# Where the row maxima of two attentions are split into bf16 parts: GpSimd or VectorE, in a planned single-core Trainium2 kernel

## The chip, the cores and the metric

The kernel runs on one core of one Trainium2 chip. The metric is the device time of one execution in microseconds (us), as the median of several runs; lower is better. One further execution was recorded by the hardware profiler, and the profile and the trace are of that one.

## The reference, cut to what matters

The input is 4096 tokens of 256 channels. After a layer norm two branches run on it, and their results are added to the input.

```python
xn = _layernorm(x)
x = x + _L0_attn_ref(xn, ...) + _L0_ffn_ref(xn, ...)

# branch 1: global attention, 16 heads of 16 channels, 4096 x 4096 scores for each head
attn = einsum('bqhd,bkhd->bhqk', q, k);  sq = attn * attn
w = sq / (nsum - 2.0 * sq + EPS)                 # nsum = |q|^2 + |k|^2
out = softmax(w) @ v

# branch 2: two layers, each a local attention (window 128, 8 heads of 64) and a gated feed-forward part
sim = where(mask, -max, bq @ bk.T);  o = softmax(sim) @ bv;  x = x + o @ wo
h = layernorm(shift_token(x)) @ w1 + b1;  a, g = split(h);  x = x + (a * gelu(g)) @ w2 + b2
```

Both softmaxes subtract the maximum of each row before the exponential. The change concerns how this maximum gets from where it is found to where it is subtracted.

## The kernel before, in words

**Global attention.** A *tile* is 128 queries of one head against all 4096 keys: 16 heads x 32 = 512 tiles, each in two *halves* of 2048 keys, each half in two pieces of 1024. The path of a half:

1. `scores` (L951): PE multiplies Q and K into PSUM; `square` (L955): ACT squares into SBUF buffer `r`, of which there are 9 (`R_BUFS`).
2. `less` (L959): VectorE subtracts 1.
3. A reciprocal by logarithm and exponential on ACT (`log` L978, `power` L981), on `u` buffers, of which there are two (`U_BUFS`). A tile takes one of two forms: *paired*, where VectorE multiplies the two halves (`product` L963), takes an absolute value (`positive` L972) and, after one logarithm and one exponential, restores the sign (`signed` L985); or *unpaired*, with `positive`, `log` and `power` once for each half. The paired form has more VectorE work, the unpaired one more ACT work.
4. `weights` (L993): one VectorE instruction for each half multiplies and finds the row maximum, followed by a short instruction that reads the accumulator into `mm`.
5. `maximum` (L1002 to L1007): the maximum, one number for each of 128 queries, is turned into three bf16 parts. The upper half of its bits is the first part; GpSimd subtracts it from the maximum (L1007), the upper half of the rest is the second part, and a second subtraction leaves the third. After each part a DMA on the SP queue (L1004) writes it as a row of `mrow`.
6. `turn` (L1014, L1017): PE transposes `r` into PSUM, having first put the negated sum of the three rows of `mrow` there (L1014). `exp` (L1025) on ACT, `values` (L1036) on PE into `pv`.
7. After four tiles `copied` (L1043) copies `pv` to `ob`, and a DMA on SP stores `ob` (L1045).

Q is loaded for four tiles at a time (`load_q`, L338), with two buffers; the load for the next four is issued at the scores of the first of a four.

**Local attention and feed-forward.** This is one long generator, `ffn` (L596 on), of which each `yield step(engine, ns, ...)` names the engine and duration of the piece that follows. A group is 256 tokens, 16 groups in each of two layers. For each of four head pairs, `looked` (L716) computes the scores, masks and scales them with a row maximum on VectorE (L740, four instructions), has GpSimd split four maxima at once into three bf16 parts in `fm3` (L745 to L748), and issues three DMAs on SP into `frow` (L751); `summed` uses them on PE (L760). `fetch(g + 1)` loads the next group's `hT` and `tab` (L631 to L638). The feed-forward part follows with 512 tokens at a time (`shifted` loads them, L824), and `finals` computes the output rows.

**What sets the order.** PE, ACT and VectorE run in an order that a planner writes down while the kernel is built: `plan_all` adds tasks with an engine, an assumed duration in ns, what they wait for, which buffers they take and give, and a rank; `Plan.run` starts, on each free engine, the ready task of lowest rank. The ranks are the tile or half number plus an offset from `RANK` (S scores, Q square, and so on). Tasks of engine `X` are no engine's: their code is emitted when their time has come. The maximum is such a task:

```python
m = add("X", MAX_NS, lambda: acts.maximum(i), 2 * i, [w])
for n in (2 * i, 2 * i + 1):
    soft(n, m)
```

so that the turn of a tile is planned `MAX_NS` after its `weights`. `load` sums the planned ACT and VectorE work, and `paired = load[0] > load[1]` chooses the form of the next tile. `ffn` is paced along by `CHAIN_NS`. GpSimd and SP are not planned: their instructions stand in about the order in which the code is emitted, and each engine runs its own in order. An instruction at the head of SP's queue that waits for its source keeps all later ones waiting.

Of the kernel before, what the change touches and what calls it, by code (L numbers as in the profile page):

```python
# [23 lines left out]
NG = S // 512  # L24
# [12 lines left out]
U_BUFS = 2  # L37
PE_BUFS = 4
PRO_LIVE = 7
CHAIN_NS = 2.5755e6  # L40

# [3 lines left out]
AFTER = {"PE": 215.0, "ACT": 178.0, "DVE": 133.0, "X": 0.0}  # L47
MODE_NS = 97.0
MODE_BONUS = 1.0
MAX_NS = 6000.0  # L50
PACE = dict(PE=1.0, ACT=0.5, DVE=0.5, X=0.0)
RANK = dict(S=-8.0, Q=-3.0, D=-2.0, L=1.5, T=1.0, W=3.0, E=5.0, P=4.5, F=5.5, O=-20.0)


class Pool:
# [127 lines left out]
def plan_all(plan, acts, chain, halves):  # L183
# [7 lines left out]
    def rest(i, subs):  # L191
        paired = load[0] > load[1]
        load[0] += 10844 if paired else 14448
        load[1] += 12321 if paired else 9050
        acts.mode(i, paired)
        add, D, L, T = plan.add, 2 * i + RANK["D"], 2 * i + RANK["L"], 2 * i + RANK["T"]
        ready = []
        if paired:
            t = add("DVE", 2203, lambda: acts.product(i), D, subs, takes=[(U, i)])
            t = add("DVE", 1135, lambda: acts.positive(i, 0), D, [], [t])  # L200
            t = add("ACT", 1802, lambda: acts.log(i, 0), L, [t])
            t = add("ACT", 1802, lambda: acts.power(i, 0), L, [t])
            ready = [add("DVE", 2203, lambda: acts.signed(i), D, [t])] * 2
        else:
            for h in range(2):
                t = add("DVE", 1135, lambda h=h: acts.positive(i, h), D + h, [subs[h]], [t] if h else [], takes=[] if h else [(U, i)])
                p = add("ACT", 1802, lambda h=h: acts.log(i, h), L + h, [t])
                ready.append(add("ACT", 1802, lambda h=h: acts.power(i, h), L + h, [p]))
        w = None
        for h in range(2):  # L210
            w = add("DVE", 2255, lambda h=h: acts.weights(i, h), T + h, [ready[h]], [w], gives=[(U, i)] if h else [])
        m = add("X", MAX_NS, lambda: acts.maximum(i), 2 * i, [w])
        for n in (2 * i, 2 * i + 1):
            soft(n, m)

    def soft(n, m):
        i, half = divmod(n, 2)
        exps = []
        for z in range(2):
            w = plan.add("PE", 427 + 8 * 109, lambda z=z: acts.turn(n, z), n + RANK["W"] + 0.3 * z, [m], [last["W"]],  # L220
                         takes=[(PS, (n, z, 1))], gives=[(R, n)] if z else [])
            last["W"] = w
            e = plan.add("ACT", 905, lambda z=z: acts.exp(n, z), n + RANK["E"] + 0.3 * z, [w], takes=[(PE2, (n, z))], gives=[(PS, (n, z, 1))])
            exps.append(e)
        fresh = [last["copy"]] if half == 0 and i % 4 == 0 else []
        last["P"] = plan.add("PE", 874, lambda: acts.values(n), n + RANK["P"], exps + fresh, [last["P"]],
                             gives=[(PE2, (n, 0)), (PE2, (n, 1))], mode="C")
        if half and i % 4 == 3:
            last["copy"] = plan.add("ACT", 465, lambda: acts.copied(i), n + RANK["O"], [last["P"]])

    def begin(n):
        sq = []
# [40 lines left out]
def tile_yat_attention_and_local_ffn(ctx: ExitStack, tc: tile.TileContext, io, out):  # L273
# [322 lines left out]
    def ffn():  # L596
        for l in range(DEPTH):
# [63 lines left out]
            for g in range(NGF):  # L661
# [42 lines left out]
                for b in range(2):  # L704
# [4 lines left out]
                                 start=k == 0, stop=k == 1)  # L709
                    yield step("DVE", 600, give=True)  # L710
                    V.tensor_copy(va[:, (2 * g + b) % 3, :, 0:FD], pv.rearrange("p (h d) -> p h d", h=FH))
                if g + 1 < NGF:
                    nxt = fetch(g + 1)
                osum = fa.tile([128, 2, INNER], F32, name="xm2")

                def looked(c):  # L716

                    P = fb.tile([128, 2, 2, 256], F32, name="P")
                    mx = fb.tile([128, 4], F32, name="mx")

                    yield step("PE", 1200, "R", take=2)
                    pss = ps_s.tile([128, 2, 2, 256], F32, name=acts.name("pt", "f"))
                    for b in range(2):
                        t = 2 * g + b
                        s0, s1 = (t - 1) % 3, t % 3
                        for j in range(1 if s1 == s0 + 1 else 2):
                            for e in range(2):
                                r = 64 * e
                                lq = qT[r:r + 64, c, b * 128:(b + 1) * 128]
                                if s1 == s0 + 1:  # L730
                                    T.matmul(pss[:, e, b].rearrange("p (s n) -> p s n", s=2), lhsT=lq,
                                             rhs=kT[r:r + 64, c, s0:s0 + 2], start=True, stop=True)
                                else:
                                    T.matmul(pss[:, e, b, j * 128:(j + 1) * 128], lhsT=lq, rhs=kT[r:r + 64, c, (s0, s1)[j]],
                                             start=True, stop=True)
                    yield step("DVE", 1620, give=2)
                    for e in range(2):
                        for b in range(2):
                            mk = msk[:, 0 if (g == 0 and b == 0) else 1]
                            V.tensor_tensor_reduce(P[:, e, b], pss[:, e, b], mk, rn[:, 0, b, 2 * c + e:2 * c + e + 1], 3.0e38,  # L740
                                                   ALU.add, ALU.min, mx[:, 2 * e + b:2 * e + b + 1])
                    yield step("X", 0)
                    m3 = fb.tile([128, 3, 4], BF, name="fm3")
                    md = fb.tile([128, 4], F32, name="fmd")
                    G.tensor_copy(m3[:, 0], mx)  # L745
                    G.tensor_tensor(m3[:, 1], mx, m3[:, 0], ALU.subtract)
                    G.tensor_tensor(md, mx, m3[:, 0], ALU.subtract)
                    G.tensor_tensor(m3[:, 2], md, m3[:, 1], ALU.subtract)  # L748
                    mT = frow[c % 2]
                    for c_ in range(3):  # L750
                        nc.sync.dma_start(mT[c_:c_ + 1], m3[:, c_])  # L751
                    held[c] = P, mT, plan.now + 10000.0

                def summed(c):
                    P, mT, at = held.pop(c)
# [27 lines left out]
                for c in range(5):  # L783
                    if c < 4:
                        yield from looked(c)
                    if c:
                        yield from summed(c - 1)
                oT = fa.tile([128, 4, GT], F32, name="qT")
# [13 lines left out]
                yield step("DVE", 600, give=True)  # L802
                xm = fa.tile([128, 2, D], F32, name="xm")
                V.tensor_tensor(xm, pw, xres, ALU.add)
                nc.sync.dma_start(xm_d[l][g * GT + 1:(g + 1) * GT + 1].rearrange("(t p) c -> p t c", p=128), xm)

            if l == DEPTH - 1:
# [21 lines left out]
            for g in range(NG):  # L829
# [13 lines left out]
                hn = fa.tile([128, 4, D], F32, name="qT")  # L843
                for t in range(4):
                    V.tensor_scalar(hn[:, t], xh[:, t], mv[:, t, 0:1], rstd[:, t:t + 1], ALU.subtract, ALU.mult)
                if g + 1 < NG:
                    nxt = shifted(g + 1)
                h2 = []
                for c in range(2):
                    yield step("PE", 510, take=True)  # L850
# [3 lines left out]
                    yield step("DVE", 725, give=True)  # L854
                    h2.append(fb.tile([128, 512], F32, name="pT"))
                    V.tensor_scalar(h2[c], ph, lngb[:, 0, c:c + 1], lngb[:, 1, c:c + 1], ALU.mult, ALU.add)
                gg = fa.tile([128, 6, 512], F32, name="kv")

                def up(s_, m):
# [36 lines left out]
                if l < DEPTH - 1:  # L896
                    for c in range(2):
# [4 lines left out]
                        yield step("DVE", 600, give=True)  # L902
                        xoT = fb.tile([128, 512], F32, name="pT")
                        V.tensor_copy(xoT, ph)
                        for z in range(2):
                            nc.sync.dma_start(xT_d[l + 1][2 * g + z][c * 128:(c + 1) * 128], xoT[:, z * GT:(z + 1) * GT])
                    for z in range(2):
                        nc.sync.dma_start(xres_d[l + 1][2 * g + z].rearrange("(t p) c -> p t c", p=128), xo[:, 2 * z:2 * z + 2])
                else:
# [2 lines left out]
                    nc.sync.dma_start(xin, acc_d[g].rearrange("(t p) c -> p t c", p=128))  # L912
                    yield step("DVE", 1135)
                    V.tensor_tensor(xo, xo, xin, ALU.add)
                    nc.sync.dma_start(ff_d[g].rearrange("(t p) c -> p t c", p=128), xo)


# [5 lines left out]
    class Acts:  # L923
# [11 lines left out]
        def scores(self, n, z):  # L935
            i, half = divmod(n, 2)
            h, qt = tiles[i]
            if half == 0 and z == 0:
                if qt == 8 and h + 1 < H:
                    assert self.valued >= 8 * NT * h  # L940
                    load_k(h + 1)
                    load_v(h + 1)
                if qt % 4 == 0 and i // 4 + 1 < len(quads):
                    load_q(*quads[i // 4 + 1])
            if z == 0:
                self.r[n] = hr.tile([128, 2048], F32, name=self.name("r", n))
# [40 lines left out]
        def weights(self, i, h):  # L987

            if h == 0:
# [3 lines left out]
            V.tensor_tensor_reduce(self.r[2 * i + h], self.r[2 * i + h], self.part(i, h), 1.0 if self.paired[i] else -0.5, init,  # L993
                                   ALU.mult, ALU.max, self.mm[i][:, h:h + 1])
            if h:
                del self.u[i]

        def maximum(self, i):

            mm = self.mm.pop(i)  # L1000
            head = mm.bitcast(BF)
            self.mT[i] = mT = mrow[i % M_ROWS]  # L1002
            for c_ in range(1, 4):
                nc.sync.dma_start(mT[c_ - 1:c_, :], head[:, 2 * c_ + 1:2 * c_ + 2])  # L1004
                if c_ == 3:
                    break
                G.tensor_tensor(mm[:, c_ + 1:c_ + 2], mm[:, c_:c_ + 1], head[:, 2 * c_ + 1:2 * c_ + 2], ALU.subtract)  # L1007

        def turn(self, n, z):
            i, half = divmod(n, 2)  # L1010
# [29 lines left out]
        def copied(self, i):  # L1040
            h, qt = tiles[i]
            self.ob = hp.tile([128, 512], F32, name="ob", bufs=1)
            A.copy(self.ob, pav)  # L1043
            if i + 1 < len(tiles):
                nc.sync.dma_start(o_d[qt // 4][h], self.ob)  # L1045
                if h == H - 1:
# [178 lines left out]
```

## Time and profile before

| | |
|---|---|
| median of 3 runs | 7337.93 us (7336.72 to 7345.24) |
| the profiled execution | 7328.83 us, of which the span of its instructions is 7327.0 us |
| busy, share of the span | ACT 95%, VectorE (DVE) 94%, PE 92%, GpSimd (POOL) 25% |
| mean granted TensorE clock | 0.981 of full speed |
| L993, VectorE, 128x2048 | 1,024 instructions, mean 2346 ns (with a start value) and 2283 ns (without) |
| L1025, ACT, 128x1024 | 2,048 instructions, mean 1099 ns |
| L1007, GpSimd, 128x1 | 1,024 instructions, mean 1010 ns, 1033.9 us in all |
| L745, L746, L747, L748, GpSimd, 128x4 | 128 each, means 1695, 1587, 1570 and 1189 ns |

Busy time is the time in which an instruction of an engine was under way; on one engine the records of two successive instructions may overlap. Idle time has a releaser: what ended the wait, as semaphores show it. SPq is the queue of DMA issues of SyncE, DVE is VectorE, POOL is GpSimd, PEld is the weight load of PE. The local attention of the two layers runs from 288 to about 2620 us and from about 3620 to 5978 us, the feed-forward parts after each; the global attention runs all along from 240 us to the end.

### The profile page before, as it was taken

The numbers are of one execution on the slowest core, as the hardware profiler recorded it, in microseconds if no ns is written. First come the engines' busy times: TensorE is split into PE (matmuls) and PEld (weight loads), VectorE is DVE, ScalarE is ACT, GpSimd is POOL, SyncE is SP. The second block draws the span as 40 slices with busy tenths as digits, with TensorE's granted clock in tenths as the row PEclk, the third lists the DMA queues.
The fourth block names the chain that finished last, engine by engine and source line by source line (L and its number), as shares of the span: only waits on it lengthen the run. The fifth ranks groups of instructions, "written<-read, shape, count | busy, mean of one in ns | idle before, by whom it ended". The sixth has DMA issues, their size and how long they took to land. (4 is left out here: it accounts for less than half of the span.)

```text
span 7327.0 us, 158565 instructions
## 1 busy us (share of the span) xinstructions
PE 6747.6 (92%) x66274; PEld 4786.4 (65%) x67136; DVE 6907.5 (94%) x7307; ACT 6972.8 (95%) x6761; POOL 1806.4 (25%) x1567
## 2 busy tenths in 40 slices
PE   7799999999999998899999999999999999999998
PEld 3466666666676665666666676666666666666665
DVE  8999999999999998899999999999999999899998
ACT  8899999999999998899999999999999999899998
POOL 0123233223332322212223322332232220011210
PEclk9899999999999999999999999999999999999999
DMA  3201010010000111011110010101010023101012
GB/s 130 76 16 21 17 24 15 17 22 17 20 19 15 30 40 26 19 31 24 35 21 19 20 19 17 23 14 25 15 23 15 17 59 87 36 21 31 20 46 77
DMA packets 542303, 223.84 MB, mean 31 GB/s; under 512 B 374988, under 2 KB 514003, under 8 KB 539538
## 3 DMA queue, kind: packets, MB, share of 16 engines
q1 hardware_dynamic: 539650, 212.73, 12.3%
q8 instruction: 527, 8.63, 0.5%
q14 instruction: 190, 1.56, 0.1%
q10 hardware_dynamic: 1936, 0.92, 0.0%
HBM read 124.59 MB, written 88.08 MB: 29 GB/s over the span
## 5 line engine op out<-in xcount | busy, mean ns | idle before, releaser
L1017 PE MATMUL pt<-ident,r 128*128 128x128 f32 x16384 | 2497.5, 276 | 0.0
L1017 PEld LDWEIGHTS pt<-ident,r 128*128 128x128 f32 x16384 | 2082.7, 143 | 577.3 <-issue 199.4
L1025 ACT ACTIVATE pe<-pt 128x1024 f32<-128x1024 f32 x2048 | 2178.8, 1099 | 147.0 <-PE pt L1017 122.5
L955 ACT ACTIVATE r<-pt 128x1024 f32<-128x1024 f32 x2048 | 2120.9, 1104 | 86.5 <-PE pt L951 45.0
L1007 POOL TENSOR_TENSOR mm<-mm 128x1 f32<-128x1 f32 x1024 | 1033.9, 1010 | 4714.3 <-DVE mm L993 4547.7
L1014 PE MATMUL pt<-mrow,neg 128*128 128x512 bf16 x4096 | 1577.6, 385 | 220.8 <-DMA mrow<-mm 108.2
L978 ACT ACTIVATE u<-u 128x2048 f32<-128x2048 f32 x702 | 1395.4, 1997 | 26.8 <-DVE u L972 26.4
L981 ACT ACTIVATE u<-u 128x2048 f32<-128x2048 f32 x702 | 1403.5, 1999 | 0.7
L959 DVE TENSOR_SCALAR r<-r 128x2048 f32<-128x2048 f32 x1024 | 1242.5, 1221 | 65.2 <-ACT r L955 64.8
L993 DVE CUSTOM_DVE_ANT_0 r<-r,u,mm 128x2048 f32<-128x2048 f32 x512 | 1201.3, 2346 | 63.4 <-ACT u L981 58.4
L951 PE MATMUL pt<-K,Q 128*128 128x512 bf16 x3234 | 1013.2, 383 | 199.7 <-ACT pe L1025 129.8
L993 DVE CUSTOM_DVE_ANT_0 r<-r,u 128x2048 f32<-128x2048 f32 x512 | 1169.1, 2283 | 13.0 <-ACT u L981 6.4
L1036 PE MATMUL pv<-pe,vh 128*17 128x128 f32 x32768 | 1074.1, 275 | 21.4 <-ACT ob L1043 7.9
L1036 PEld LDWEIGHTS pv<-pe,vh 128*17 128x17 f32 x32768 | 819.0, 97 | 298.7 <-issue 279.7
L985 DVE SCALAR_TENSOR_TENSOR u<-u 128x2048 f32<-128x2048 f32 x322 | 736.1, 2286 | 74.6 <-ACT u L981 73.8
L951 PEld LDWEIGHTS <-Q 128*128 128x128 bf16 x4096 | 375.4, 99 | 574.6 <-issue 393.6
L963 DVE TENSOR_TENSOR u<-r,r 128x2048 f32<-128x2048 f32 x322 | 735.6, 2285 | 1.9
L1014 PEld LDWEIGHTS <-neg 128*128 128x128 bf16 x4096 | 406.7, 99 | 350.7 <-issue 249.6
L972 DVE TENSOR_SCALAR u<-r 128x2048 int32<-128x2048 int32 x380 | 457.1, 1219 | 1.6 <-DMA q_d<-pb 1.5
L972 DVE TENSOR_SCALAR u<-u 128x2048 int32<-128x2048 int32 x322 | 394.4, 1225 | 7.5
L863 PE MATMUL pf<-pT,wqkv_s 128*128 128x512 f32 (+1 forms) x768 | 367.5, 601 | 4.2 <-DVE kv L883 1.5
L745 POOL CAST fm<-mx 128x4 bf16<-128x4 f32 x128 | 216.9, 1695 | 481.2 <-DVE mx L740 470.5
(211 smaller groups left out, 6005.1 us busy)
## 6 DMA issues: line engine op xcount, KB each, us to landing
o<-ob SPq DMA_DIRECT2D x127, 256.0 KB
mrow<-mm SPq DMA_DIRECT2D x1536, 0.2 KB
Q<-q_d SPq DMA_DIRECT2D x256, 48.0 KB
K<-k_d SPq DMA_DIRECT2D x32, 384.0 KB
tab<-in_tables_dram SPq DMA_DIRECT2D x32, 256.0 KB
xres<-xres SPq DMA_DIRECT2D x32, 256.0 KB
xm<-xm SPq DMA_DIRECT2D x32, 256.0 KB
P<-xm SPq DMA_DIRECT2D x32, 256.0 KB
```

Of the source, the lines that this page charges most:

```text
L951: T.matmul(ps[:, j * 512:(j + 1) * 512], lhsT=Q[:, (qt % 4) * 128:(qt % 4 + 1) * 128], rhs=K[:, o + j * 512:o + (j + 1) * 512], start=True ...
L955: A.activation(self.r[n][:, z * 1024:z * 1024 + 1024], self.pt.pop((n, z)), AF.Square)
L959: V.tensor_scalar(self.r[n], self.r[n], 1.0, 1.0e-9, ALU.subtract, ALU.subtract)
L972: V.tensor_scalar(self.part(i, h).bitcast(I32), src.bitcast(I32), 0x7FFFFFFF, None, ALU.bitwise_and)
L978: A.activation(self.part(i, h), self.part(i, h), AF.Ln)
L981: A.activation(self.part(i, h), self.part(i, h), AF.Exp, scale=-2.0)
L993: V.tensor_tensor_reduce(self.r[2 * i + h], self.r[2 * i + h], self.part(i, h), 1.0 if self.paired[i] else -0.5, init, ALU.mult, ALU.max, ...
L1007: G.tensor_tensor(mm[:, c_ + 1:c_ + 2], mm[:, c_:c_ + 1], head[:, 2 * c_ + 1:2 * c_ + 2], ALU.subtract)
L1014: T.matmul(pt[:, 512 * b:512 * b + 512].rearrange("p (s n) -> p s n", s=4), lhsT=neg1, rhs=self.mT[i].unsqueeze(1).broadcast_to([128, 4, 1 ...
L1017: T.matmul(pt[:, 512 * b + j * 128:512 * b + (j + 1) * 128], lhsT=self.r[n][:, o + j * 128:o + (j + 1) * 128], rhs=ident, is_transpose=Tru ...
L1025: A.activation(pe, self.pt.pop((n, z)), AF.Exp)
L1036: T.matmul(pav[32 * (j % 4):32 * (j % 4) + 17, (qt % 4) * 128:(qt % 4) * 128 + 128], lhsT=vh[h % 2][:, kt, :], rhs=pe[:, j * 128:(j + 1) * ...
```

## The change

The bf16 parts of both maxima are made on VectorE, directly behind the instruction that finds the maximum: in `weights` two subtractions of 128x1 after the second half, in `looked` two subtractions of 128x4 and one copy of all twelve parts. GpSimd does nothing in either attention any more. The DMAs stay on SP. Several DMA issues move to a later place in the emitted order: the store of `ob` into a step of its own (`stored`), the next Q to the second tile of a four, `fetch(g + 1)` behind the second head pair, `shifted(g + 1)` behind the transposes, and the stores of `xm`, `xoT` and `ff` behind a step `X` that ends after the VectorE instruction that makes them. The planner's numbers follow: 145 ns for the pair and 240 ns for the three of `looked`, `MAX_NS` 5000 for 6000, ranks of S and Q lower, `CHAIN_NS` larger.

```diff
-CHAIN_NS = 2.5755e6
+CHAIN_NS = 2.6012e6
-MAX_NS = 6000.0
+MAX_NS = 5000.0
-RANK = dict(S=-8.0, Q=-3.0, D=-2.0, L=1.5, T=1.0, W=3.0, E=5.0, P=4.5, F=5.5, O=-20.0)
+RANK = dict(S=-13.0, Q=-3.5, D=-2.0, L=1.5, T=1.0, W=3.0, E=5.0, P=4.5, F=5.5, O=-20.0)
...
-        load[1] += 12321 if paired else 9050
+        load[1] += 12466 if paired else 9195
...
-            w = add("DVE", 2255, lambda h=h: acts.weights(i, h), T + h, [ready[h]], [w], gives=[(U, i)] if h else [])
+            w = add("DVE", 2255 + 145 * h, lambda h=h: acts.weights(i, h), T + h, [ready[h]], [w], gives=[(U, i)] if h else [])
...
             last["copy"] = plan.add("ACT", 465, lambda: acts.copied(i), n + RANK["O"], [last["P"]])
+            plan.add("X", 0, lambda: acts.stored(i), n, [last["copy"]])
...
-                if g + 1 < NGF:
-                    nxt = fetch(g + 1)
                 osum = fa.tile([128, 2, INNER], F32, name="xm2")
...
-                    mx = fb.tile([128, 4], F32, name="mx")
+                    mx = fb.tile([128, 3, 4], F32, name="mx")
...
-                    yield step("DVE", 1620, give=2)
+                    yield step("DVE", 1860, give=2)
...
+                    m3 = fb.tile([128, 3, 4], BF, name="fm3")
+                    hd = mx.bitcast(BF).rearrange("p j (n w) -> p j n w", w=2)[:, :, :, 1]
+                    for c_ in range(2):
+                        V.tensor_tensor(mx[:, c_ + 1], mx[:, c_], hd[:, c_], ALU.subtract)
+                    V.tensor_copy(m3, hd)
                     yield step("X", 0)
-                    m3 = fb.tile([128, 3, 4], BF, name="fm3")
-                    md = fb.tile([128, 4], F32, name="fmd")
-                    G.tensor_copy(m3[:, 0], mx)
-                    G.tensor_tensor(m3[:, 1], mx, m3[:, 0], ALU.subtract)
-                    G.tensor_tensor(md, mx, m3[:, 0], ALU.subtract)
-                    G.tensor_tensor(m3[:, 2], md, m3[:, 1], ALU.subtract)
                     mT = frow[c % 2]
                     for c_ in range(3):
                         nc.sync.dma_start(mT[c_:c_ + 1], m3[:, c_])
-                    held[c] = P, mT, plan.now + 10000.0
+                    held[c] = P, mT, plan.now + 8000.0
...
                         yield from looked(c)
+                    if c == 1 and g + 1 < NGF:
+                        nxt = fetch(g + 1)
...
                 V.tensor_tensor(xm, pw, xres, ALU.add)
+                yield step("X", 0)
                 nc.sync.dma_start(xm_d[l][g * GT + 1:(g + 1) * GT + 1].rearrange("(t p) c -> p t c", p=128), xm)
...
-                if qt % 4 == 0 and i // 4 + 1 < len(quads):
+                if qt % 4 == 1 and i // 4 + 1 < len(quads):
                     load_q(*quads[i // 4 + 1])
...
             if h:
+                mm, head = self.mm[i], self.mm[i].bitcast(BF)
+                for c_ in range(1, 3):
+                    V.tensor_tensor(mm[:, c_ + 1:c_ + 2], mm[:, c_:c_ + 1], head[:, 2 * c_ + 1:2 * c_ + 2], ALU.subtract)
                 del self.u[i]
...
             for c_ in range(1, 4):
                 nc.sync.dma_start(mT[c_ - 1:c_, :], head[:, 2 * c_ + 1:2 * c_ + 2])
-                if c_ == 3:
-                    break
-                G.tensor_tensor(mm[:, c_ + 1:c_ + 2], mm[:, c_:c_ + 1], head[:, 2 * c_ + 1:2 * c_ + 2], ALU.subtract)
...
+        def stored(self, i):
+            h, qt = tiles[i]
             if i + 1 < len(tiles):
                 nc.sync.dma_start(o_d[qt // 4][h], self.ob)
```

In the built programs the order on PE, ACT and VectorE is written anew by the planner throughout; the counts of PE's instructions and of SP's DMAs are the same, ACT has 32 more, VectorE 1,392 more, and GpSimd 36 instead of 1,572.

More of the change, by code (lines that the diff above doesn't have):

```diff
@@ L740, in looked @@
                             V.tensor_tensor_reduce(P[:, e, b], pss[:, e, b], mk, rn[:, 0, b, 2 * c + e:2 * c + e + 1], 3.0e38,
-                                                   ALU.add, ALU.min, mx[:, 2 * e + b:2 * e + b + 1])
-                    yield step("X", 0)
-                    m3 = fb.tile([128, 3, 4], BF, name="fm3")
-                    md = fb.tile([128, 4], F32, name="fmd")
-                    G.tensor_copy(m3[:, 0], mx)
-                    G.tensor_tensor(m3[:, 1], mx, m3[:, 0], ALU.subtract)
-                    G.tensor_tensor(md, mx, m3[:, 0], ALU.subtract)
-                    G.tensor_tensor(m3[:, 2], md, m3[:, 1], ALU.subtract)
+                                                   ALU.add, ALU.min, mx[:, 0, 2 * e + b:2 * e + b + 1])
+                    m3 = fb.tile([128, 3, 4], BF, name="fm3")
[3 more added lines that the diff above has]
+                    V.tensor_copy(m3, hd)
+                    yield step("X", 0)
                     mT = frow[c % 2]
@@ L845, in ffn @@
                     V.tensor_scalar(hn[:, t], xh[:, t], mv[:, t, 0:1], rstd[:, t:t + 1], ALU.subtract, ALU.mult)
-                if g + 1 < NG:
-                    nxt = shifted(g + 1)
                 h2 = []
@@ L856, in ffn @@
                     V.tensor_scalar(h2[c], ph, lngb[:, 0, c:c + 1], lngb[:, 1, c:c + 1], ALU.mult, ALU.add)
+                if g + 1 < NG:
+                    nxt = shifted(g + 1)
                 gg = fa.tile([128, 6, 512], F32, name="kv")
@@ L904, in ffn @@
                         V.tensor_copy(xoT, ph)
+                        yield step("X", 0)
                         for z in range(2):
@@ L914, in ffn @@
                     V.tensor_tensor(xo, xo, xin, ALU.add)
+                    yield step("X", 0)
                     nc.sync.dma_start(ff_d[g].rearrange("(t p) c -> p t c", p=128), xo)
```

## Prediction

> **What bounds the kernel now.** I read the page's busy line first, then the busy time by stretch, the waits, and three pieces of the timeline. Columns of the second fence: stretch and its length, then PE, PEld, DVE, ACT and POOL busy.
>
> ```profile
> PE 6747.6 (92%) x66274; PEld 4786.4 (65%) x67136; DVE 6907.5 (94%) x7307; ACT 6972.8 (95%) x6761; POOL 1806.4 (25%) x1567
> ```
>
> ```profile
> 300.00:2650.00 2350.00, 2194.10 (x22659) 1608.81 (x22949) 2264.48 (x2455) 2295.79 (x2279) 693.46 (x603) 0.99 0.10 20
> 2650.00:3600.00 950.00, 872.61 (x8099) 593.60 (x8201) 855.85 (x796) 873.68 (x772) 211.65 (x133) 0.97 0.11 26
> 3600.00:5900.00 2300.00, 2147.62 (x22210) 1577.17 (x22508) 2211.80 (x2380) 2244.65 (x2228) 659.21 (x585) 0.99 0.10 20
> 5900.00:7290.00 1390.00, 1288.19 (x12202) 877.38 (x12360) 1288.91 (x1226) 1309.09 (x1157) 229.16 (x214) 0.98 0.18 48
> ```
>
> No engine waits for one other all the time: ACT and VectorE are both nearly full. I call stretches one and three (global attention beside the local attention) A: 4650 us, ACT idle 109.6, VectorE idle 173.7. Stretches two and four (beside the feed-forward part and the final rows) are B: 2340 us, ACT idle 157.2, VectorE 195.2, PE 179.2. So A is bound by ACT, with VectorE only 64 us behind it; B by several engines in turn.
>
> ```profile
> ACT pe L1025 <- PE pt L1017: 122.5, 105, 9.9
> ...
> PE pt L1014 <- DMA mrow<-mm: 108.2, 38, 8.8
> ...
> PEld L1014 <- DMA mrow<-mm: 44.7, 15, 9.3
> ```
>
> ```profile
> 2818.68 17.87 SPq L1004 DMA_DIRECT2D mrow<-mm  x3
> 2818.70 18.63 POOL L1007 TENSOR_TENSOR mm<-mm 128x1 f32<-128x1 f32 x4 [13.92 <-DVE mm L993]
> ...
> 2838.92 0.61 PE L1014 MATMUL pt<-mrow,neg 128*128 128x512 bf16 x1 [8.85 <-DMA mrow<-mm]
> ```
>
> The first fence is waits (us in total, times, longest), the second a piece of the timeline. This is the stall that the change is about: the maximum's second and third parts come from GpSimd, each followed by its DMA on SP, and PE's turn L1014 waits for the third landing; ACT's exponential then waits for PE. Summing the gaps from 2 us before to 12 us after each such wait, ACT idles 61 us in A and 56 us in B, VectorE 59 and 46. That is all that the stalls hold.
>
> ```profile
> L1007 POOL TENSOR_TENSOR mm<-mm x1024: 189/1057/11197, 262.9 to 7297.8; 128x1 f32<-128x1 f32 x171
> ```
>
> ```profile
> L959 DVE TENSOR_SCALAR r<-r x1024: 1203/1220/2339, 241.4 to 7273.7; 128x2048 f32<-128x2048 f32 x171
> ```
>
> Minimum, median, maximum in ns: the GpSimd subtraction takes 189 ns alone and usually ends with the VectorE instruction beside it, so its time is waiting. L959 takes a median 1220 ns both where a GpSimd operation overlaps it and where none does (522 and 502 instances). The Trainium skill (SBUF — State Buffer, "Who interferes with whom") states an exclusive lock that fully blocks whichever of the two comes second; here only GpSimd is seen to pay. By the rule taken both ways, removing 1,536 operations would give VectorE up to 1,536 x 0.19 = 290 us, ACT would stay the bound and the sum would end near 7295. By the rows of L959 I take nothing for the port.
>
> **What VectorE gets.** Counted in the two built programs: 1,024 subtractions of 128x1, 256 of 128x4 and 128 copies of 128x12 come to VectorE, in 512 + 128 places, for 1,024 + 512 operations of GpSimd. The first subtraction waits for the accumulator read just before it, the second for the first, the copy for the second. No row shows this on VectorE; four show its pieces.
>
> ```profile
> 14.14 0.16 DVE L403 TENSOR_TENSOR tm<-tm,ve 128x4 f32<-128x4 f32 x1
> 14.22 0.15 DVE L348 SCALAR_TENSOR_TENSOR ex<-ex,ex 128x3 f32<-128x3 f32 x1
> ```
>
> ```profile
> 394.63 0.18 DVE L778 RECIPROCAL inv<-pf 128x4 f32<-128x4 f32 x1
> 394.85 0.42 DVE L779 TENSOR_TENSOR xm<-pf,inv 128x256 f32<-128x256 f32 x1
> ```
>
> ```profile
> 4007.57 0.08 DVE L993 DVE_READ_ACCUMULATOR2_ANT mm<- 128x1 f32 x1
> 4007.69 2.35 DVE L993 CUSTOM_DVE_ANT_0 r<-r,u,mm 128x2048 f32<-128x2048 f32 x1
> 4009.97 0.08 DVE L993 DVE_READ_ACCUMULATOR2_ANT mm<- 128x1 f32 x1
> 4009.97 0.48 DVE L740 CUSTOM_DVE_ANT_0 P<-pt,msk,rn 128x256 f32<-128x256 f32 x1
> ```
>
> Small independent operations start 0.07 us apart although each lasts 0.15: they overlap. L779 reads what L778 writes, and starts 0.035 us after its end, 0.21 after its start. After an accumulator read the next instruction starts at +0.00 if independent (L740) and at +0.12 if it reads the result (L993). So a tile's split costs 0.12 + 0.15 + 0.035 + 0.07 = 0.37 us (the plan says 145 ns), and a local-attention split 0.12 + 2 x 0.19 + 0.07 = 0.57 us (the plan: 240 ns). The lower bound, with no dependent wait, is 0.145 and 0.22. I take the upper values, because a dependent pair is what stands there.
>
> The Trainium skill (VectorE: DVE Perf Modes, "The DRAIN you can't avoid") holds that the next operation waits for the pipe in any case and that a semaphore in between costs nothing. The starts at 14.14 and 394.85 disagree with it. By that rule the split would be at its lower bound, the faster rival below.
>
> **The balance.** The plan sends 16 of 322 paired tiles to the form with more ACT work (306 remain). One such tile takes 2 x 2.20 - 1.14 = 3.27 us from VectorE (starts of L963, L985, L972) and gives ACT 2 x 1.80 = 3.60 us (L978, L981): 12 in A, 4 in B. In all VectorE gets 512 x 0.37 + 128 x 0.57 - 52 = +211 us and ACT +58 us.
>
> **Stage A** holds 342 tiles and 125 local splits. VectorE's work becomes 4476.3 + 126.5 + 71.3 - 39.2 = 4634.9 us, ACT's 4540.4 + 43.2 = 4583.6. VectorE is now the bound. Today's bound engine there, ACT, idles 49 us away from the stalls; I give VectorE the same, and leave a quarter of the 61 us of stalls (15): 4699 us, **+49 us**. Ends: no residue from stalls 4684, all of it 4745.
>
> **Stage B** holds 166 tiles, 3 local splits: VectorE +50 us, ACT +14. Three quarters of ACT's 56 us come back (-42); half of VectorE's growth lands on the path (+25), the rest in its idle 195 us: **-17 us**, with ends -56 and +50.
>
> **The turn.** Today the third part's DMA is issued 1.25 us after the maximum at the least, 2.36 at the median, 10.4 or more at the worst stalls in B; PE goes on about 2.9 us after that issue in the shortest such waits. With VectorE the parts are there after 0.37 us, and SP's three issues (0.6 us each) decide: some 1.3 + 2.9 = 4.2 us. The plan places the turn 5.0 us after the maximum instead of 6.0, so the slack (0.8 us) is that of today's median (6.0 - 5.3); only the tail goes. Hence the quarter kept: three Q issues (1.86 us for three at 2836.64) or a 0.75 to 1.5 us store of o ahead of a row on SP still exceed it.
>
> **Stores, Q, fetches** are issues on SP, none added. SP stood waiting at its head for ob (249.0 us, 67 times), for PE before Q (227.6, 62 times), for hT and tab of the fetch (94.5 and 103.3). Moving these later frees the rows behind them, which is inside the stall gain already. Cover of what moves: a fetch still has two of four head pairs of its 145 us group (4650 us for 32); Q three tiles of 13.6 us instead of four; ob is rewritten four tiles on. I cost them at 0; if the fetch's cover were gone, 32 groups x 4 us (197.8 us of such waits in 49) = 128 us. The copy into fm3 now waits on VectorE for the frow DMAs of two steps ago, with all VectorE work behind it; GpSimd waited 10.6 us there, so 0 to 11, and I take 0, since the step that consumed those rows comes first. Ranks: scores stand 16.7 pieces of 1024 columns ahead of the turns in the old order and 16.8 in the new, so I take 0.
>
> **Sum.** +49 - 17 = +32 us on the profiled execution's 7328.8 (span 7327.0 plus 1.8 around it): 7361. The median of the runs stands 9 us above that execution, so 7338 + 32 = **7370**. About 0.2% (15 us) is what a measurement tells from no change: 7323 to 7353.
>
> **Rivals.** *Faster:* dependent waits do not show (0.145 and 0.22), and VectorE stays under ACT. A: VectorE 4514, ACT 4583.6 + 49 + 15 = 4648 (-2); B -42 + 6 = -36. That is 7300, and 7271 if no stall stays. It decides from about 0.31 us per split (sum zero: A's VectorE work 4603). Against it: every dependent pair shown; for it: the margin is thin, 32 us of 198.
> *VectorE's growth is not absorbed:* with two u buffers it passes tiles back and forth with ACT, so each late split delays the logarithm behind it. +211, less three quarters of ACT's 117 us of stalls: +123, 7461. For it: waits of VectorE for ACT's u, 73.8 and 64.9 us; against: B's idle time.
> *The change doesn't do what it says:* SP's order, not GpSimd, holds the rows, and all stalls stay: A 4634.9 + 110 (+95), B +25: 7458. Against it: SP's waits at L1004 and L751 end mostly with POOL instructions.
>
> **Chances.** Forecast 0.45 (own range 7340 to 7405; 0.12 of it inside the band of no change), faster rival 0.28, the two that end far above 0.15 and 0.12. Faster 0.28, same 0.12, slower 0.60. The ends of A and B alone span 7316 to 7483; the range reaches into the faster rival and those two, 7280 to 7455, which leaves out about 2 in 10.
>
> **What would show it.** Right: starts of accumulator read, first and second subtraction 0.12 and 0.19 us apart; VectorE's idle in A falling to some 65 us with ACT's above it; waits of PE for mrow at a quarter; L959 still at 1220 ns. Wrong: the two subtractions 0.07 us apart, VectorE still idler than ACT in A, or PE's waits for mrow as long as now.

## The result, and the profile after

The changed kernel takes 7391.1 us, against 7337.3 us for the kernel before: a ratio of 1.008, with a 95% interval of 1.0067 to 1.0092. It is slower, as forecast (7370, range 7280 to 7455). The profiled execution took 7391.5 us with a span of 7389.3, so its span is 62.3 us longer than before. The busy line of the page, after:

```profile
PE 6821.3 (92%) x67136; PEld 4770.1 (65%) x67136; DVE 7066.5 (96%) x8699; ACT 7045.0 (95%) x6793; POOL 10.8 (0%) x31
```

GpSimd's 1806 us of busy time are gone, and VectorE has 159 us more: it is now the fullest engine. (The trace before lacks 862 of PE's score matmuls; the program has as many as after.) Busy time by stretch (PE, PEld, VectorE, ACT, POOL, then granted clock, DMA share and GB/s):

```profile
300.00:2650.00 2350.00, 2185.68 (x22569) 1579.44 (x22569) 2286.40 (x2937) 2283.79 (x2252) 1.13 (x1) 0.99 0.10 20
2650.00:3600.00 950.00, 906.10 (x8532) 608.81 (x8532) 903.25 (x971) 907.05 (x804) 0.00 (x0) 0.99 0.12 28
3600.00:5900.00 2300.00, 2144.21 (x22213) 1548.07 (x22212) 2239.35 (x2853) 2242.11 (x2211) 3.07 (x3) 1.00 0.10 20
5900.00:7290.00 1390.00, 1292.68 (x12153) 867.99 (x12152) 1297.27 (x1422) 1302.84 (x1153) 0.20 (x1) 0.98 0.19 46
```

In the first and third stretch VectorE is now as full as ACT; before, it was 32 us emptier in each. In the second both are 33 to 47 us fuller: there PE no longer waits for the rows of the maximum, for which it waited 31 us before. These windows are fixed in time and hold more or fewer tiles from kernel to kernel. So from here on a stage is counted from one tile's maximum to another's (tiles 3 to 176 and 243 to 412 for A, 176 to 243 and 412 to 511 for B), with the sums taken from the trace:

| span of the stage, us | before | after | change | predicted |
|---|---|---|---|---|
| A (342 tiles, beside the local attention) | 4648.8 | 4728.5 | +79.7 | +49 |
| B (166 tiles, feed-forward and final rows) | 2346.0 | 2326.6 | -19.4 | -17 |
| start and end | 332.2 | 334.3 | +2.1 | 0 |

The waits, in total, times, longest:

```profile
PE pt L1017 <- DMA mrow<-mm: 110.3, 88, 11.7
...
ACT pe L1028 <- PE pt L1020: 103.0, 124, 7.4
...
PEld L1017 <- DMA mrow<-mm: 54.2, 27, 12.6
```

The wait for the rows of the maximum has not become shorter in total (108.2 and 44.7 before). It has become other waits: 88 where there were 38, and more than half of them under 1 us. A wait of PE and one of its weight load can be the same time; counted once, it is 124 us, 113 before (82 and 57 in A, 29 and 52 in B). The third DMA is now issued 1.28 us after the maximum at the median instead of 2.36, and 4.6 us at the most instead of 17.5.

One of these waits, from the accumulator read that ends the maximum to the turn:

```profile
1247.31 0.08 DVE L996 DVE_READ_ACCUMULATOR2_ANT mm<- 128x1 f32 x1
...
1247.42 1.76 SPq L1010 DMA_DIRECT2D mrow<-mm  x3
...
1253.34 0.38 PE L1017 MATMUL pt<-mrow,neg 128*128 128x512 bf16 x1 [1.01 <-DMA mrow<-mm]
```

Here the turn starts 5.95 us after the maximum (1247.39 to 1253.34). In the 65 of the 88 waits whose third DMA was issued within 1.4 us, it starts 5.8 us after the maximum at the least and 6.0 at the median. The plan puts it at 5.0. PE had ended its work before the turn, and so could have begun it, within 6.0 us of the maximum in 113 of the 512 tiles, against 13 before.

The split on VectorE, from the timeline:

```profile
4017.47 0.08 DVE L996 DVE_READ_ACCUMULATOR2_ANT mm<- 128x1 f32 x1
4017.59 0.35 DVE L1002 TENSOR_TENSOR mm<-mm 128x1 f32<-128x1 f32 x2
4017.86 0.48 DVE L739 CUSTOM_DVE_ANT_0 P<-pt,msk,rn 128x256 f32<-128x256 f32 x1
...
4019.48 0.09 DVE L739 DVE_READ_ACCUMULATOR2_ANT mx<- 128x1 f32 x1
4019.60 0.36 DVE L744 TENSOR_TENSOR mx<-mx 128x4 f32<-128x4 f32 x2
4019.99 0.17 DVE L745 COPY fm<-mx 128x12 bf16<-128x12 bf16 x1
4020.07 2.28 DVE L966 TENSOR_TENSOR u<-r,r 128x2048 f32<-128x2048 f32 x1
```

From the accumulator read to the next independent instruction a pair takes 0.39 us (17.47 to 17.86) and a local split 0.59 us (19.48 to 20.07): 0.37 and 0.57 had been predicted, 0.145 and 0.24 planned. Two source answers (minimum, median, maximum in ns):

```profile
L1002 DVE TENSOR_TENSOR mm<-mm x1024: 158/159/163, 263.2 to 7360.0; 128x1 f32<-128x1 f32 x171
```

```profile
L962 DVE TENSOR_SCALAR r<-r x1024: 1205/1219/2337, 240.7 to 7340.3; 128x2048 f32<-128x2048 f32 x171
```

With GpSimd silent, VectorE's 128x2048 subtraction takes 1219 ns, against 1220 before.

### The profile page after: what moved, and what is told of

Read it like the earlier page. It is cut to its first block, busy times and chain, and to the rows that moved or that the text cites. A ratio compares the mean times of both kernels' runs of the same rounds, so it can differ in the third digit from the quotient of the medians.

```text
span 7389.3 us, 157765 instructions
## 1 busy us (share of the span) xinstructions
PE 6821.3 (92%) x67136; PEld 4770.1 (65%) x67136; DVE 7066.5 (96%) x8699; ACT 7045.0 (95%) x6793; POOL 10.8 (0%) x31
## 3 DMA queue, kind: packets, MB, share of 16 engines
q14 instruction: 177, 1.45, 0.1%
## 4 chain that ended last, share of the span: by engine, by line
DVE 48%; ACT 25%; PE 15%; issue 6%; DMA 5%; SPq 1%; DVEq 0%; ACTq 0%
DVE r L996 18%; DVE r L962 7%; ACT pe L1028 6%; ACT r L958 6%; ACT u L984 5%; DVE u L975 5%; DVE u L988 5%; DVE u L966 4%; ACT u L981 4%; DMA mrow<-mm 4%; PE pt L1020 4%; PE pt L1017 2%; DVE P L739 2%; PE pv L1039 2%; PE pt L954 2%
## 5 line engine op out<-in xcount | busy, mean ns | idle before, releaser
L1028 ACT ACTIVATE pe<-pt 128x1024 f32<-128x1024 f32 x2048 | 2120.3, 1075 | 116.7 <-PE pt L1020 103.0
L958 ACT ACTIVATE r<-pt 128x1024 f32<-128x1024 f32 x2048 | 2088.4, 1078 | 56.7 <-PE pt L954 55.2
L962 DVE TENSOR_SCALAR r<-r 128x2048 f32<-128x2048 f32 x1024 | 1238.7, 1220 | 65.9 <-ACT r L958 65.7
L954 PE MATMUL pt<-K,Q 128*128 128x512 bf16 x4096 | 1140.1, 382 | 172.9 <-ACT pe L1028 126.0
L988 DVE SCALAR_TENSOR_TENSOR u<-u 128x2048 f32<-128x2048 f32 x306 | 698.9, 2284 | 31.4 <-ACT u L984 31.1
L966 DVE TENSOR_TENSOR u<-r,r 128x2048 f32<-128x2048 f32 x306 | 698.8, 2284 | 0.9
L975 DVE TENSOR_SCALAR u<-r 128x2048 int32<-128x2048 int32 x412 | 497.0, 1219 | 1.5 <-DMA q_d<-pb 1.5
L975 DVE TENSOR_SCALAR u<-u 128x2048 int32<-128x2048 int32 x306 | 374.4, 1224 | 7.1
L677 PE MATMUL pf<-wqkv_s,hT 128*128 128x512 f32 x512 | 246.1, 603 | 7.2 <-ACT kv L699 4.0
L772 PEld LDWEIGHTS pf<-kv,pT 128*128 128x128 f32 x2048 | 240.5, 192 | 16.3 <-ACT pT L766 9.5
```

The lines of the kernel that those rows point to most:

```text
L954: T.matmul(ps[:, j * 512:(j + 1) * 512], lhsT=Q[:, (qt % 4) * 128:(qt % 4 + 1) * 128], rhs=K[:, o + j * 512:o + (j + 1) * 512], start=True ...
L958: A.activation(self.r[n][:, z * 1024:z * 1024 + 1024], self.pt.pop((n, z)), AF.Square)
L962: V.tensor_scalar(self.r[n], self.r[n], 1.0, 1.0e-9, ALU.subtract, ALU.subtract)
L975: V.tensor_scalar(self.part(i, h).bitcast(I32), src.bitcast(I32), 0x7FFFFFFF, None, ALU.bitwise_and)
L988: V.scalar_tensor_tensor(z, z, -0.5, self.u[i][:, 0:2048], ALU.mult, ALU.mult)
L1028: A.activation(pe, self.pt.pop((n, z)), AF.Exp)
```

## The experiments

Ratios are to the kernel before, run beside each experiment on the same chip; its median there lay between 7333.0 and 7338.3 us. By the intervals, two experiments that differ by less than about 12 us are not told apart. Two causes were to be told apart: VectorE's own time, and the way in which the new plan times the turn against SP's queue.

**The moved DMAs alone** (`e1_moves`): all moves of stores, Q and fetches on the kernel before.

> The kernel before with the moved stores, Q loads and fetches alone; both splits stay on GpSimd, the planner's numbers are the old ones. Theory (VectorE's own time is what the change costs): 7315 to 7340 us, since the moves only free SP's queue. Rival (the new order of the DMAs is at fault): above 7360 us.

7336.0 us, ratio 1.0003 (0.9994 to 1.0013): nothing. SP stands at its head as before, for instance for PE before Q (246.6 us in 68 waits, 227.6 in 62 before) and for `ob` (249.0 us in 67 waits before):

```profile
SPq L1052 <- ACT ob L1047: 252.7, 73, 10.2
```

**The splits alone** (`e2_split`): the two VectorE splits with the planned 145 and 240 ns on the kernel before.

```diff
+                    V.tensor_tensor(mm[:, c_ + 1:c_ + 2], mm[:, c_:c_ + 1], head[:, 2 * c_ + 1:2 * c_ + 2], ALU.subtract)
-                G.tensor_tensor(mm[:, c_ + 1:c_ + 2], mm[:, c_:c_ + 1], head[:, 2 * c_ + 1:2 * c_ + 2], ALU.subtract)
```

> The kernel before with both splits on VectorE and their planned 145 and 240 ns alone; DMAs where they were, MAX_NS 6000, old ranks. Theory (VectorE's time): slower by about as much as the whole change, 7375 to 7410 us, VectorE's idle time beside the local attention at 65 us or less in each half. Rival (the turn planned 1 us earlier, which meets SP's queue in many short waits, is the cost): 7320 to 7350 us, as the turn is planned late here.

7353.3 us, ratio 1.0024 (1.0013 to 1.0035): between the two expectations. Slower, but by less than a third of the whole change. A is 4684.9 us (+36), B 2315.0 (-31), start and end 352.5 (+20); VectorE idles 96 us in A and ACT 101. The waits of PE for the rows are all but gone (17.8 and 10.3 us; 22 counted once). So the rest of the change's loss lies in MAX_NS, the ranks, CHAIN_NS, the local attention's planned lead (8 us in place of 10, the line with `plan.now`), or what they do together.

**The turn 6.0 us after the maximum again** (`e4_max6`).

```diff
-MAX_NS = 5000.0
+MAX_NS = 6000.0
```

> The changed kernel with MAX_NS at 6000 again and nothing else. Theory (VectorE's time): the waits of PE for mrow fall from 111 us to under 40, but the time stays, 7380 to 7405 us. Rival (short planned turn): most of the loss goes, 7330 to 7355 us.

7364.0 us, ratio 1.0037 (1.0023 to 1.0051): half of the loss goes, which lies between the two expectations; PE's row of waits falls to 63 us, not under 40. **The old ranks** (`e8_ranks`), with the turn at 5.0 us:

```diff
-RANK = dict(S=-13.0, Q=-3.5, ...
+RANK = dict(S=-8.0, Q=-3.0, ...
```

> The changed kernel with the old ranks of scores and squares (S -8, Q -3). If the lower ranks are a part of the loss (scores pushed ahead of turns on PE): 7365 to 7382 us. If only VectorE's time and the turn's lead count: 7385 to 7397 us.

7361.6 us, ratio 1.0032 (1.0020 to 1.0045): again half, more than either expectation had. Either of the two taken back leaves A at 4697 or 4691 us, where the prediction had it (4699). The waits of PE in the two, first with MAX_NS 6000, then with the old ranks:

```profile
PE pt L1017 <- DMA mrow<-mm: 62.6, 48, 11.2
...
PEld L1017 <- DMA mrow<-mm: 43.3, 23, 12.1
```

```profile
PE pt L1017 <- DMA mrow<-mm: 59.8, 55, 6.1
...
PEld L1017 <- DMA mrow<-mm: 23.0, 17, 4.4
```

So the shorter lead and the lower ranks do not add. In A the one puts 6 us on top of `e2_split`, the other 13, both together 44; B, start and end together differ by 7 us at most among these four. The moves, CHAIN_NS and the shorter local lead are in all but `e2_split`, and the last two were not tried by themselves. The third DMA's issue is the same in all of them (median 1.28 us after the maximum); what differs is when PE comes to the turn. It could have begun it within 6.0 us of the maximum in 29 of 512 tiles in `e2_split`, in 67 with the old ranks, in 63 with MAX_NS 6000, and in 113 in the changed kernel. By which tasks PE comes there earlier was not tried.

**The planner told the true price** (`e5_true`): 390 and 580 ns in place of 145 and 240.

> The changed kernel with the planner told the measured price of the splits (390 ns for the pair instead of 145, 580 ns instead of 240); 283 paired tiles instead of 306. First theory (VectorE's unplanned 0.25 and 0.34 us make it the late engine): VectorE gives up 75 us to ACT, 7360 to 7380 us. Second theory (the turn planned after 5.0 us is what costs): within 8 us of the change's 7391.

7388.8 us, ratio 1.0068 (1.0053 to 1.0083): no gain on the change. With 283 paired tiles instead of 306, VectorE has idle time again in A (157 us) and ACT next to none (55), and A is shorter (4697.5 us); but B takes 2339.4, 13 us more, and start and end 15 more. The first theory missed and the second held: the balance between the two engines is not what is wrong.

**Other work between the dependent operations, in the changed kernel** (`e3_nowait`): each subtraction and copy a planned VectorE step of its own.

> The changed kernel with the same subtractions and copies on VectorE, each as a planned step of its own, so that other VectorE work stands between a result and the next operation that reads it. Theory (the dependent waits are the larger half of the price): 174 us of VectorE time come back (512 x 0.25 + 128 x 0.36), stage A falls back to ACT's bound, 7300 to 7345 us. Rival (short planned turn against SP's queue): the parts come later still, so 7385 us or more.

7347.9 us, ratio 1.0016 (1.0007 to 1.0026): 43 us less than the change, just outside the expectation, and as to stage A it is right (4623.9 us, 25 under the kernel before). B grows to 2391 us. **The same on the split kernel** (MAX_NS 6000, old ranks), for the global pair alone (`e7_glob`) and for the local one too (`e9_both`):

```diff
+        for c_ in (1, 2):
+            w = add("DVE", 72, lambda c_=c_: acts.split(i, c_), 2 * i - 20, [w])
         m = add("X", MAX_NS, lambda: acts.maximum(i), 2 * i, [w])
```

> The kernel before with both splits on VectorE, MAX_NS 6000 and old ranks (as in e2_split), but the two subtractions of the global attention as planned steps of their own, with other VectorE work in between; the local split stays in one piece. First theory: 128 us of VectorE's waits go (512 x 0.25), which is worth some 40 us in time, 7300 to 7330 us, faster than before. Second theory (the parts come 2 to 3 us later and the turn waits): 7345 us or more.

7288.5 us, ratio 0.9933 (0.9918 to 0.9947): faster than the kernel before, 65 us under `e2_split`, and faster than the first theory had it. The timeline shows what the steps do:

```profile
4000.24 0.08 DVE L994 DVE_READ_ACCUMULATOR2_ANT mm<- 128x1 f32 x1
4000.24 1.22 DVE L960 TENSOR_SCALAR r<-r 128x2048 f32<-128x2048 f32 x1
4001.38 0.15 DVE L1001 TENSOR_TENSOR mm<-mm 128x1 f32<-128x1 f32 x1
4001.45 1.22 DVE L960 TENSOR_SCALAR r<-r 128x2048 f32<-128x2048 f32 x1
4002.58 0.15 DVE L1001 TENSOR_TENSOR mm<-mm 128x1 f32<-128x1 f32 x1
4002.65 2.28 DVE L964 TENSOR_TENSOR u<-r,r 128x2048 f32<-128x2048 f32 x1
```

The same two subtractions now take 0.07 us each (1.38 to 1.45, 2.58 to 2.65): 0.14 in place of 0.39. The price is delay: the third DMA is issued 2.97 us after the maximum at the median.

> As e7_glob, and the local attention's two subtractions and copy are planned steps of their own too. First theory: another 46 us of VectorE's waits go (128 x 0.36), 7290 to 7325 us. Second theory (each step more makes the chain of the local attention longer, so that more of it is left for the end): slower than e7_glob by 10 us or more, with the loss in the stretch from 5900 us on.

7314.2 us, ratio 0.9971 (0.9959 to 0.9983): slower than `e7_glob` by 26 us, as the second theory had it, though the first's range holds the time too. A is 34 us shorter, B 65 longer, about half of that before 5900 us and half after. Spread out, the local split adds steps to a chain in which each waits for the last, and the chain falls behind. Last starts of the local maximum, without and with its steps spread out:

```profile
L742 DVE CUSTOM_DVE_ANT_0 P<-pt,msk,rn x512: 471/477/485, 353.1 to 5931.6; 128x256 f32<-128x256 f32 x171
```

```profile
L742 DVE CUSTOM_DVE_ANT_0 P<-pt,msk,rn x512: 466/478/485, 355.3 to 6019.6; 128x256 f32<-128x256 f32 x171
```

**Is it the waits, or the longer lead?** In `e7_glob` the lead counts from the second subtraction, so the turn stands some 8.5 us after the maximum. `e10_lead` is `e2_split` with `MAX_NS = 8500.0`.

> As e2_split (7353 us), with the turn planned 8.5 us after the maximum, about where e7_glob's extra steps put it. First theory (the dependent waits on VectorE were e2_split's loss, and e7_glob's gain is their going): 7335 to 7358 us. Rival (e7_glob gained by the longer lead of the turn): 7285 to 7310 us.

7362.0 us, ratio 1.0034 (1.0022 to 1.0046): no gain, and not told apart from `e2_split`, though 4 us above the first theory's range. PE is free for the turn 10.3 us after the maximum at the median, 10.6 in `e7_glob` and 8.7 in `e2_split`, so the lead is there. It alone is not `e7_glob`'s gain: `e2_split` had only 22 us of waits for the rows to lose. That leaves the waits on VectorE as its loss. **The same lead on the kernel before** (`e11_pool_lead`), splits on GpSimd and not one instruction moved to another engine:

```diff
-MAX_NS = 6000.0
+MAX_NS = 8500.0
```

> The kernel before, splits on GpSimd, with the turn planned 8.5 us after the maximum and nothing else. If the stalls behind GpSimd were worth their idle time (117 us of ACT's) and a longer lead hides them: 7250 to 7300 us, and the splits need not move at all. If a longer lead only fills the r buffers and moves the stall elsewhere: 7325 to 7350 us.

7265.0 us, ratio 0.9898 (0.9883 to 0.9912): the fastest of all. Its busy line and its waits for the rows:

```profile
PE 6793.7 (94%) x67136; PEld 4759.6 (66%) x67136; DVE 6903.9 (95%) x7307; ACT 6970.0 (96%) x6761; POOL 1736.5 (24%) x1567
```

```profile
PE pt L1014 <- DMA mrow<-mm: 61.7, 24, 11.6
...
PEld L1014 <- DMA mrow<-mm: 16.3, 7, 5.8
```

GpSimd is as slow as ever (third issue 2.36 us after the maximum at the median, 5.4 us at nine in ten), and nearly half of the stalls are gone nonetheless: PE waits 64 us, counted once, where it waited 113. A takes 4606.4 us (-42) and B 2319.6 (-26). ACT's idle time in A falls from 106 to 66 us while VectorE does no more than before. No other lead was tried on this kernel.

**The dose** (`e12_twice`): `e2_split` with the global pair made twice.

> As e2_split, with the global pair of subtractions made twice, to the same values; the planner is told nothing of it. It adds 512 x 0.39 = 200 us to VectorE and 0.4 us to the third part's way. If VectorE's time lands on the path one for one: 7540 us; if half of it: 7450 us; if it is absorbed: under 7380 us.

7519.6 us, ratio 1.0245 (1.0228 to 1.0262): +166 us for 200 us of VectorE, nearer to one for one than to half. In A it is +122 for 133 (342 x 0.39), in B +44 for 65. By the busy line VectorE has 163 us more than the 7067 of `e2_split`, PE 35 and ACT 16 more:

```profile
PE 6863.6 (91%) x67136; PEld 4780.2 (64%) x67136; DVE 7229.7 (96%) x9725; ACT 7051.3 (94%) x6789; POOL 7.5 (0%) x31
```

**Balance in the interleaved kernel** (`e13_balance`): 313 paired tiles.

> As e7_glob, with half of the global split's 145 ns in the planner's balance, so 313 paired tiles and not 306: ACT gets 25 us less, VectorE 23 us more. ACT idled least in e7_glob, so 7275 to 7290 us if ACT is the bound there; 7290 to 7310 us if both are.

7284.6 us, ratio 0.9925 (0.9910 to 0.9940), not to be told from `e7_glob`. Most of these experiments also have a new order on PE, ACT and VectorE, as the planner writes it. What a new order does by itself was not tested; with seven tiles in the other form it did next to nothing here.

## Why the prediction was right, and where not

- **The price of a split** (0.37 and 0.57 us, with dependent waits): right, 0.39 and 0.59, and the planner's 145 and 240 ns were too low. In A, VectorE's busy time plus the 34 ns gaps inside the splits is about 4634 us, the sum predicted (4634.9).
- **That these waits decide the sign**: shown for the split kernel. With the same operations and other work between them it goes from 1.0024 to 0.9933; a longer lead without that gives 1.0034. In the changed kernel they do not decide it alone: `e3_nowait` is at 1.0016, still slower than before. The Trainium skill (VectorE: DVE Perf Modes, "The DRAIN you can't avoid") has a wait between two operations cost nothing, from a test of eight copies. Here the same subtraction costs about 0.2 us behind its source and 0.07 us behind other work, so for operations this short the measurement decides against it. The same section says that an operation which is not held starts earlier than the emptied pipe; the prediction left that out, and the independent starts 0.07 us apart agree with it.
- **No gain from the freed port**: right for L962 (1219 ns, 1220 before). The exclusive lock of the Trainium skill (SBUF — State Buffer, "Who interferes with whom") agrees with GpSimd's side alone: its subtraction took 189 ns at the least and 1057 at the median, and VectorE's 128x2048 subtraction did not pay.
- **The balance**: 16 tiles changed form as counted; ACT's busy time grew by 72 us where 58 were predicted.
- **Stage B**: -17 predicted, -19 measured. ACT's idle time there fell by 32 us, where returned stalls alone were to give 42; whether each of the two terms was right was not tested.
- **Stage A**: +49 predicted, +80 measured. The term that failed is the turn's: 1.3 + 2.9 = 4.2 us from the maximum until the rows can be used, and with it "so the slack (0.8 us) is that of today's median (6.0 - 5.3); only the tail goes", with a quarter of the stalls kept. The 1.3 was right (1.28). The 2.9 was not: PE goes on 4.75 us after the third issue at the median, 6.0 us after the maximum, so a turn planned at 5.0 comes about 1 us too early and there is no slack. The trace before held both values: PE went on 2.9 us after the third issue where that was 1.5 us or more behind the second (15 waits, median), and 4.9 us where it was less than 0.7 us behind (14 waits). VectorE's parts, ready at once, make the second kind the rule. The tail of the DMA issues did go (17.5 to 4.6 us), but the stalls stayed, which the prediction had named as a sign of being wrong: 124 us for 113, in A 82 for 57. VectorE's idle time in A is 129 us, or 93 without the gaps inside the splits, where 65 was named. The ranks at 0 failed with it: taking back either the lead or the ranks puts A near the predicted 4699 (4691 and 4697 us), so the two together were worth about 30 us more than the prediction gave them. The time lies in the forecast's range nonetheless, because the upper end given for A (4745) lets all the stalls stay.
- **Stores, Q and fetches at 0**: right, 1.0003 (0.9994 to 1.0013) by themselves; but not because they free the rows behind them, as the text said. SP waits at the same places for about as long.
- **The rivals.** The faster one had its mechanism right and its premise wrong: `e7_glob` is what it described, once the waits are taken out by order. The one in which VectorE's growth is not absorbed is close to what the dose shows (0.83 of each added us), but the first 210 us met slack and returned stalls. The one in which SP's order keeps all the stalls had the amount right, but not the cause: `e2_split`, with SP's issues where they were, has 22 us of them.
- **What the text had not seen**: nearly half of the stalls were a matter of the planned lead. The kernel before had room for 2.5 us more of it, and with that the slow GpSimd chain cost less than any split on VectorE tried here.

## What to carry to other kernels

Before moving small work from an idle slow engine to a full fast one to shorten its latency, try giving the latency more room in the schedule: here one number (6.0 to 8.5 us) brought 1.0% where the move lost 0.8%. If small dependent operations must go on a full engine, put independent work between them, for a dependent one costs nearly three times an interleaved one. Measure how long a value takes with its transfers as close together as they will be, and plan no shorter lead. And retune leads and priorities one at a time against the kernel at hand: two that cost 6 and 13 us of stage A alone cost 44 together.

## What was not expected of the hardware

- A VectorE pair of 128x1 subtractions costs 0.39 us in one piece and 0.14 us with 128x2048 instructions in between.
- On an engine 96% busy, 200 us of added work lengthened the span by 166 us, though ACT was as busy.
- SP's wait at the head for `ob` or Q did not become shorter when these issues moved to a later place in the emitted order (249 and 253 us for `ob`, 228 and 247 for Q), and the third row's DMA was issued as long after the maximum as before (median 2.36 us in both).
- Of three small DMAs issued 0.6 us apart, the rows could be used 4.75 us after the third issue (median of 65 waits); with 1.5 us or more between the last two, 2.9 us after it (15 waits of the kernel before).
